# User stage in chunks of 20 history positions, transposed by VectorE in 32x32 blocks and placed by SBUF-to-SBUF DMAs, in place of groups of 4 positions transposed by TensorE

## The chip, the cores and the metric

The kernel runs on one core of one Trainium2 chip. The metric is the device time of one execution in microseconds (us); it was measured three times for the kernel before, between 31807.33 and 31812.54 us, with a median of 31807.57 us. One more execution was profiled, and all rows below come from that one.

The engines are named as in the profile: PE is TensorE (matrix products), PEld its loading of weights, DVE is VectorE, ACT is ScalarE, POOL is GpSimd, and SP is SyncE, which here only issues DMAs. A `q` behind an engine's name marks its sequencer, which issues a DMA while the engine itself stays idle.

## The reference, cut to what matters

```python
V = E[near_full]                       # 50001 items, 32 neighbours each
a_sus, a_inf = attention(E_in), attention(E_out)     # per item, over its neighbours
h = concat([E_hist[history], a_sus[history], a_inf[history]])   # 16384 x 100 x 128
t = concat([E_tgt[target], a_inf[target], a_sus[target]])       # 16384 x 128
x = h * t[:, None, :]
z = relu(einsum('bld,hd->blh', x, W1) + b1)                     # 128 -> 128
scores = einsum('blh,h->bl', z, W2[0])
exp_A = exp(scores) * ((history != target[:, None]) & (history != 0))
attn = exp_A / sum(exp_A, -1) ** 0.5
s = sum(h * attn[..., None])           # one number over everything
pred = dot(s, t) / (|s| * |t|);  return sigmoid(pred)
```

Everything is fp32. The output is one number for each of 16384 users.

## The kernel before, in words

There are two long stages and a short end.

**Neighbour stage** (lines 119 to 270). For each of 391 tiles of 128 items, POOL issues 32 indirect DMAs (line 161); each gathers one row of 64 numbers into each of 128 partitions, by an index that lies in SBUF. VectorE forms products (176), sums (183), weighted values (209) and weighted sums (217) in batches of two tiles; ScalarE takes the exponentials. The rows that result go to a table in HBM, 129 numbers for an item: the row's sum and the 128 numbers of `h`. The change leaves this stage as it is, save the width of the small constant `pick`.

**User stage** (lines 272 to 464). The users stand in 128 tiles of 128 (UC = 128), each user in a partition. A tile has 100 history positions, and for each of them one indirect DMA (line 343) gathers 128 rows of 516 bytes from the table, one for each partition. Four positions are a group (LG = 4), 25 groups make a tile, and step `s` runs over all 3200 groups:

- `gather(s)`: four indirect DMAs into the row buffer `rows[s % HB]`, one of HB = 6. The first waits until the transposes of step s - 6 have read that buffer.
- `sums(s)`: VectorE copies the four row sums to `hsum` (369), after the last of the four gathers has landed.
- `turn(s - 2)`: TensorE transposes four 128x128 blocks into PSUM (361).
- `times_target(s - 2)`: VectorE multiplies the PSUM block by the transposed target `tT` and writes `xT` to SBUF (378). One of its inputs lies in PSUM, the other in SBUF.
- `hidden`, `relu`, `scored`: TensorE multiplies by W1 (388), ScalarE takes the relu (394), TensorE picks the score of each position into a PSUM bank that collects the 25 groups (404).
- `weights`, `exponents`, `ended`: once per tile the bank is copied, transposed and passed through the exponential; four VectorE instructions of 100 columns mask and sum (428 to 431). Those on lines 428 and 430 have both inputs in SBUF, and so has line 333 of `target_work`.

`target_rows` gathers the target's rows for the next tile (310), `target_work` prepares the target, its sums and the mask (316 to 337).

**The order** on each engine is the order in which the code is written (`manual_schedule`), and each engine takes its instructions in turn. POOL carries no arithmetic: its queue is 12512 gathers on line 161, then 128 on line 310 among 12800 on line 343. Every gather signals its landing on one of eight semaphores in turn, and waits for the landing of the one eight places ahead of it. `after` adds a wait; `covered` drops one that a later wait or an engine's order makes needless.

Of the kernel before, what the change touches and what calls it, by code (L numbers as in the profile page):

```python
# [15 lines left out]
ALU = mybir.AluOpType  # L16
# [27 lines left out]
LG = 4  # L44
NG = L // LG
W = 1 + D
M = 2
HB = 6
RP = 3
LH = 3  # L50
LS = 6
LEAD = 2
XB = 5
ZB = 5

# [3 lines left out]
def kernel(  # L59
# [34 lines left out]
    pick = const.tile([HID, NG, NG], F32, name="pick")  # L94
# [26 lines left out]
    rows = [u_h.tile([P, LG, W], F32, name=f"h{i}") for i in range(HB)]  # L121
# [150 lines left out]
    with (  # L272
        tc.manual_schedule(engines={E.PE, E.Activation, E.DVE, E.SP, E.Pool}),
        tc.tile_pool(name="u_r", bufs=1) as u_r,
        tc.tile_pool(name="u_s", bufs=3) as u_s,
        tc.tile_pool(name="ps_r", bufs=1, space=bass.MemoryType.PSUM) as ps_r,
    ):
        users = {}
        landed, turned, times, first, second, third, copied = {}, {}, {}, {}, {}, {}, {}
        hT = [ps_r.tile([P, LG, P], F32, name=f"hT{i}") for i in range(RP)]  # L280
        z_ps = [ps_r.tile([HID, LG, P], F32, name=f"z_ps{i}") for i in range(RP)]
        writers, at = [], {}

        def next_bank():
            writers.append([])
            return hT[(len(writers) - 1) % RP]

        def writes(one):
            writers[-1].append(one)
            if len(writers) > RP:  # L290
                for other in writers[len(writers) - 1 - RP]:
                    covered(one, other)
            return one
        bank = [ps_r.tile([NG, LG, P], F32, name=f"bank{i}") for i in range(2)]
        xT = [u_r.tile([D, LG, P], F32, name=f"xT{i}") for i in range(XB)]
        z = [u_r.tile([HID, LG, P], F32, name=f"z{i}") for i in range(ZB)]
# [21 lines left out]
        def target_work(c):  # L318
            u = users[c]
            t = u["t"]  # L320
            tT_ps = next_bank()
            writes(nc.tensor.transpose(tT_ps[:, 0, :], t, ident))  # L322
            tT = u_t.tile([D, 1, P], F32, name="tT")
            nc.vector.tensor_copy(tT[:, 0, :], tT_ps[:, 0, :])
            u["tT"] = tT
            nc.vector.tensor_reduce(tsum[:, c : c + 1], t, AX.X, ALU.add)
            junk = u_t.tile([P, D], F32, name="junk")
            nc.scalar.activation(junk, t, AF.Square, accum_out=tsq[:, c : c + 1])
            keep = u_s.tile([P, L], F32, name="keep")
            idf = u_s.tile([P, L], F32, name="idf")  # L330
# [8 lines left out]
        def gather(s):  # L339
            c, g = divmod(s, NG)  # L340
            for q in range(LG):
                l = g * LG + q
                got = landed[s, q] = nc.gpsimd.indirect_dma_start(  # L343
                    out=rows[s % HB][:, q, :],
                    out_offset=None,
                    in_=table,
                    in_offset=bass.IndirectOffsetOnAxis(
                        ap=users[c]["hidx"][:, l : l + 1], axis=0
                    ),
                )  # L350
                if s >= HB:
                    if q == 0:
                        after(got, turned[s - HB, LG - 1])
                    if q < LG - 1:
                        covered(got, turned.pop((s - HB, q)))

        def turn(s):
            at[s] = next_bank()
            for q in range(LG):
                turned[s, q] = writes(  # L360
                    nc.tensor.transpose(at[s][:, q, :], rows[s % HB][:, q, 1:W], ident)  # L361
                )
            for q in range(LG):
                covered(turned[s, q], landed[s, q])
            after(turned[s, 0], copied[s])

        def sums(s):
            c, g = divmod(s, NG)
            copied[s] = copy = nc.vector.tensor_copy(  # L369
                users[c]["hsum"][:, g * LG : (g + 1) * LG],  # L370
                rows[s % HB][:, :, 0:1].rearrange("p q o -> p (q o)"),
            )
            for q in range(LG - 1):
                covered(copy, landed[s, q])

        def times_target(s):
            c, g = divmod(s, NG)
            times[s] = nc.vector.tensor_tensor(  # L378
                xT[s % XB], at.pop(s), users[c]["tT"].to_broadcast([D, LG, P]), ALU.mult
            )  # L380
            for q in range(LG - 1):
                covered(times[s], turned[s, q])
            if s >= XB:
                covered(times[s], times[s - XB])
                covered(times[s], first[s - XB])

        def hidden(s):
            first[s] = nc.tensor.matmul(z_ps[s % RP], w1T, xT[s % XB], start=True, stop=True)  # L388
            if s >= RP:
                covered(first[s], first[s - RP])  # L390
                after(first[s], second[s - RP])

        def relu(s):
            second[s] = nc.scalar.activation(z[s % ZB], z_ps[s % RP], AF.Relu, bias=b1_sb)  # L394
            if (s + LH + 1, LG - 1) in turned:
                covered(second[s], first[s])
                after(second[s], turned[s + LH + 1, LG - 1])
            if s >= ZB:
                covered(second[s], second[s - ZB])
                covered(second[s], third[s - ZB])  # L400

        def scored(s):
            c, g = divmod(s, NG)
            third[s] = nc.tensor.matmul(  # L404
                bank[c % 2], pick[:, g, :], z[s % ZB], start=g == 0, stop=g == NG - 1
            )

        def weights(c):
            flat = u_t.tile([NG, LG, P], F32, name="flat")
            copy = nc.scalar.copy(flat, bank[c % 2])  # L410
            for g in range(NG - 1):
                covered(copy, third[c * NG + g])
            users[c]["flat"] = flat

        def exponents(c):
            flat = users[c].pop("flat")
            score = next_bank()
            for q in range(LG):
                writes(nc.tensor.transpose(score[:, q, 0:NG], flat[:, q, :], ident[0:NG, 0:NG]))
            users[c]["ea"] = u_s.tile([P, L], F32, name="ea")  # L420
            nc.scalar.activation(
                users[c]["ea"].rearrange("p (g q) -> p q g", q=LG), score[:, :, 0:NG], AF.Exp
            )

        def ended(c):
            u = users.pop(c)
            ea = u["ea"]
# [5 lines left out]
        last = UC * NG  # L433
        target_rows(0)
        target_work(0)
        for s in range(last + LEAD + LS + 6):
            c, g = divmod(s, NG)
            if s < last:
                if g == 0 and c % BSUB == 2 and 0 < c // BSUB and c // BSUB + 1 < UC // BSUB:
                    history_of(c // BSUB + 1)  # L440
                if g == 5 and c + 1 < UC:
                    target_rows(c + 1)
                gather(s)
                sums(s)
            r = s - LEAD
            if 0 <= r < last:
                turn(r)
            if 0 <= r - LH < last:
                hidden(r - LH)
            if 0 <= r - LH - 1 < last:  # L450
                relu(r - LH - 1)
# [92 lines left out]
```

## Time and profile before

| what | us |
|---|---|
| median of three runs | 31807.57 |
| lowest and highest run | 31807.33, 31812.54 |
| span of the profiled execution, first to last instruction | 31804.2 |
| busy in that span: PE / DVE / ACT / POOL | 10552.2 / 6968.9 / 2748.7 / 24002.5 |
| mean granted TensorE clock | 0.907 |

The profiled execution's own time is known by its span; the median of the three runs lies 3.4 us above that span.

A row of the page reads: line, engine, operation, output<-inputs by the program's names, shape, count, then the busy time of all of them in us and the mean of one in ns, and behind the bar the engine's idle time just ahead of them with what ended most of it. "Issue" stands for an idle time in which the engine waited for nothing that the profile shows. A row of the timeline reads: start in us, duration in us, engine, line, operation, tiles, and in brackets the idle time just ahead of it.

### The profile page before, as it was taken

To read this page: it belongs to the slowest core of one execution; us is meant where nothing else is said; L and a number is where in the kernel's file an instruction comes from. 1 tells how busy PE (TensorE), PEld (TensorE's weight loads), DVE (VectorE), ACT (ScalarE), POOL (GpSimd) and SP (SyncE) were. 2 spreads that over 40 slices of the span, in tenths; PEclk is the share of its full clock that TensorE was granted. 3 is DMA by queue.
4 is the path that set the end of the run, shared out by engine and by line. 5 is a ranking of instruction groups with operands and counts; after the bars stand their busy time and mean duration, and the time that the engine had idled before them with its cause. 6 is when DMAs were issued, how large, how long until landed. Compare 5 with 4: busy or idle time off the path is not lost.

```text
span 31804.2 us, 99297 instructions
## 1 busy us (share of the span) xinstructions
PE 10552.2 (33%) x26243; PEld 3265.1 (10%) x26243; DVE 6968.9 (22%) x9965; ACT 2748.7 (9%) x5698; POOL 24002.5 (75%) x25446
## 2 busy tenths in 40 slices
PE   0000000000000000000166666666666666666666
PEld 0000000000000000000022222222222222222222
DVE  2222222222222222222211111111111111111111
ACT  0000000000000000000011111111111111111111
POOL 7777777777777777777777777777777777777777
PEclk9999999999999999999988888888888888888888
DMA  2111111111111111111122222222222222222222
GB/s 51 30 30 30 30 30 34 30 30 30 30 30 34 30 30 30 30 30 32 37 54 54 54 54 54 54 54 54 54 54 54 54 54 54 54 54 54 54 53 52
DMA packets 1027929, 1361.99 MB, mean 43 GB/s; under 512 B 559905, under 2 KB 614433, under 8 KB 1027361
## 3 DMA queue, kind: packets, MB, share of 16 engines
q0 software_dynamic: 814080, 1265.42, 16.5%
q1 hardware_dynamic: 112800, 51.60, 0.6%
q10 hardware_dynamic: 100480, 38.63, 0.6%
q8 instruction: 206, 3.38, 0.0%
q14 instruction: 363, 2.97, 0.0%
HBM read 1315.31 MB, written 51.50 MB: 43 GB/s over the span
## 4 chain that ended last, share of the span: by engine, by line
POOL 61%; issue 27%; DMA 12%; DVE 0%; POOLq 0%; PE 0%; ACT 0%; DVEq 0%; ACTq 0%
POOL v L161 36%; POOL h L343 25%; DMA h<-table,hidx 10%; DMA v<-in_egeo_dram,nidx 2%; POOL t L310 0%; POOLq L343 0%; DVE xT L378 0%; DVE den L429 0%; PE bank L404 0%; DVE ea L428 0%; PE z_ps L388 0%; DVE wv L209 0%; POOLq L161 0%; DMA nidx<-in_near_dram 0%; DVE hsum L369 0%
## 5 line engine op out<-in xcount | busy, mean ns | idle before, releaser
L343 POOL DMA_INDIRECT h<-table,hidx x12800 | 12076.8, 943 | 3901.3 <-issue 3493.5
L161 POOL DMA_INDIRECT v<-in_egeo_dram,nidx x12512 | 11804.3, 943 | 3820.7 <-issue 3756.2
L322 PE MATMUL hT<-ident,t 128*128 128x128 f32 x128 | 45.2, 353 | 15631.0 <-DMA t<-ttab,tidx 15631.0
L388 PE MATMUL z_ps<-xT,w1T 128*128 128x512 f32 x6400 | 4508.2, 796 | 0.0
L361 PE MATMUL hT<-ident,h 128*128 128x128 f32 x12800 | 2518.4, 329 | 5597.1 <-DVE hsum L369 4686.9
L404 PE MATMUL bank<-z,pick 128*25 128x512 f32 x6400 | 4231.8, 750 | 0.0
L369 DVE COPY hsum<-h 128x4 f32<-128x4 f32 x3200 | 616.7, 193 | 13349.4 <-DMA h<-table,hidx 13349.4
L394 ACT ACTIVATE z<-z_ps,b_sb 128x512 f32<-128x512 f32 x3200 | 2198.8, 687 | 13530.0 <-PE hT L361 13525.8
L176 DVE TENSOR_TENSOR prod<-v,own_ps 128x4096 f32<-128x4096 f32 x196 | 864.5, 4411 | 10996.4 <-DMA v<-in_egeo_dram,nidx 10996.4
L361 PEld LDWEIGHTS hT<-ident,h 128*128 128x128 f32 x12800 | 1597.8, 161 | 9101.8 <-DVE hsum L369 7555.2
L378 DVE TENSOR_TENSOR xT<-hT,tT 128x512 f32<-128x512 f32 x3200 | 2174.4, 680 | 0.0
L322 PEld LDWEIGHTS hT<-ident,t 128*128 128x128 f32 x128 | 18.9, 147 | 15774.4 <-issue 15772.8
L193 ACT ACTIVATE ex<-sc,top 128x32 f32<-128x32 f32 x782 | 227.7, 291 | 14840.8 <-DVE top L188 14821.9
L209 DVE TENSOR_TENSOR wv<-v,ex 128x1024 f32<-128x1024 f32 x782 | 1377.0, 1872 | 355.9 <-ACT ex L193 355.9
L388 PEld LDWEIGHTS z_ps<-xT,w1T 128*128 128x128 f32 x6400 | 1232.0, 239 | 2.6 <-ACT z L394 2.5
L183 DVE TENSOR_REDUCE sc<-prod 128x128 f32<-128x4096 f32 x196 | 864.4, 4410 | 6.7
L217 DVE TENSOR_REDUCE att<-wv 128x128 f32<-128x4096 f32 x196 | 864.1, 4409 | 6.1
L404 PEld LDWEIGHTS bank<-z,pick 128*25 128x25 f32 x6400 | 459.2, 115 | 3494.6 <-issue 3494.6
L310 POOL DMA_INDIRECT t<-ttab,tidx x128 | 120.7, 943 | 55.0 <-issue 37.5
L193 ACT ACTIVATION_READ_ACCUMULATOR ex<-sc,top 128x1 f32 x782 | 146.0, 187 | 0.0
L174 ACT COPY own_ps<-own 128x64 f32<-128x64 f32 x391 | 82.3, 210 | 60.4 <-DVE row L235 54.3
L220 DVE TENSOR_TENSOR row<-att,tot 128x64 f32<-128x64 f32 x391 | 70.7, 222 | 6.7
(53 smaller groups left out, 789.7 us busy)
## 6 DMA issues: line engine op xcount, KB each, us to landing
h<-table,hidx POOLq DMA_INDIRECT x12800, 2.5
v<-in_egeo_dram,nidx POOLq DMA_INDIRECT x12512, 2.4
table<-row ACTq DMA_DIRECT2D x22, 1096.5 KB, 13.4
own<-in_egeo_dram SPq DMA_DIRECT2D x23, 544.0 KB, 8.4
row<-in_ehist_dram SPq DMA_DIRECT2D x23, 544.0 KB, 4.7
ttab<-in_etgt_dram ACTq DMA_DIRECT2D x1, 12500.0 KB, 54.1
ttab<-row SPq DMA_DIRECT2D x22, 544.0 KB, 4.4
hidx<-in_history_dram SPq DMA_DIRECT2D x32, 200.0 KB, 2.4
```

The costliest lines, as they stand in the source:

```text
L161: nc.gpsimd.indirect_dma_start(out=v[:, m, k].rearrange("p t d -> p (t d)"), out_offset=None, in_=egeo, in_offset=bass.IndirectOffsetOnAxi ...
L176: nc.vector.tensor_tensor(prod[:, 0:n].rearrange("p m k t d -> p m k (t d)"), v.rearrange("p m k t d -> p m k (t d)"), own_ps[:, 0:n].to_b ...
L183: nc.vector.tensor_reduce(sc[:, 0:n].rearrange("p m t k -> p m k t"), prod[:, 0:n], AX.X, ALU.add)
L209: nc.vector.tensor_tensor(wv[:, m, t].rearrange("p d k -> p k d"), subs[b]["v"][:, m, :, t, :], ex[:, m, t, :].rearrange("p (k o) -> p k o ...
L217: nc.vector.tensor_reduce(att[:, 0:n], wv[:, 0:n], AX.X, ALU.add)
L343: got = landed[s, q] = nc.gpsimd.indirect_dma_start(out=rows[s % HB][:, q, :], out_offset=None, in_=table, in_offset=bass.IndirectOffsetOn ...
L361: nc.tensor.transpose(at[s][:, q, :], rows[s % HB][:, q, 1:W], ident)
L369: copied[s] = copy = nc.vector.tensor_copy(users[c]["hsum"][:, g * LG : (g + 1) * LG], rows[s % HB][:, :, 0:1].rearrange("p q o -> p (q o)"),)
L378: times[s] = nc.vector.tensor_tensor(xT[s % XB], at.pop(s), users[c]["tT"].to_broadcast([D, LG, P]), ALU.mult)
L388: first[s] = nc.tensor.matmul(z_ps[s % RP], w1T, xT[s % XB], start=True, stop=True)
L394: second[s] = nc.scalar.activation(z[s % ZB], z_ps[s % RP], AF.Relu, bias=b1_sb)
L404: third[s] = nc.tensor.matmul(bank[c % 2], pick[:, g, :], z[s % ZB], start=g == 0, stop=g == NG - 1)
```

## The change

The user stage is written anew; the neighbour stage and the end stay. A step is now a chunk of 20 positions (LQ = 20), five for each tile of users, 640 in all.

- `gather(s)` issues the same indirect DMAs in the same order, 20 in a row, into one of three row buffers of 20 positions.
- `blocks(s)` has three VectorE instructions: `x = h * t` over 20 x 128 columns (343 of the new file; both inputs lie in SBUF, the target's row repeated over the 20 positions), the copy of 20 row sums (349), and one transpose of all 32x32 blocks of `x` into `xb` (357).
- `move(s)` has SyncE issue 16 DMAs within SBUF, each of 32 partitions times 640 columns, which put block (a, b) into its place in `xT`.
- `hidden`, `relu`, `scored` take groups of 512 columns as before, five for a chunk; `relu` takes two at once. TensorE transposes nothing in this stage any more.
- `weights`: VectorE transposes the bank of scores in 32x32 blocks, four DMAs place them; then the exponential and the same four VectorE instructions. The target is no longer transposed.

```diff
-LG = 4
-NG = L // LG
+LQ = 20
+NCH = L // LQ
+Q = 4
+GS = 32
+COLS = 512
+NG = L * P // COLS
+PER = NG // NCH
-HB = 6
-RP = 3
-LH = 3
-LS = 6
-LEAD = 2
-XB = 5
-ZB = 5
+HB = 3
+XB = 2
+ZB = 4
+LS = 4
...
-    rows = [u_h.tile([P, LG, W], F32, name=f"h{i}") for i in range(HB)]
+    rows = [u_h.tile([P, LQ, W], F32, name=f"h{i}") for i in range(HB)]
...
-                if s >= HB:
-                    if q == 0:
-                        after(got, turned[s - HB, LG - 1])
...
+        def blocks(s):
+            c, k = divmod(s, NCH)
+            u = users[c]
+            h = rows[s % HB]
+            x = u_x.tile([P, LQ, D], F32, name="x")
+            made = nc.vector.tensor_tensor(
+                x,
+                h[:, :, 1:W],
+                u["t"].rearrange("p (o d) -> p o d", o=1).to_broadcast([P, LQ, D]),
+                ALU.mult,
+            )
+            copy = nc.vector.tensor_copy(
+                u["hsum"][:, k * LQ : (k + 1) * LQ], h[:, :, 0:1].rearrange("p q o -> p (q o)")
+            )
...
+            xb = xbs[s % XB]
+            turn = nc.vector.transpose(
+                xb.rearrange("p b q j -> p q b j"), x.rearrange("p q (b i) -> p q b i", b=Q)
+            )
+            if s >= XB:
+                after(copy, first.pop(s - XB))
...
+        def move(s):
+            xb = turned.pop(s)
+            xT = u_m.tile([D, Q, LQ * GS], F32, name="xT")
+            went[s] = [
+                nc.sync.dma_start(
+                    xT[b * GS : (b + 1) * GS, a, :],
+                    xb[a * GS : (a + 1) * GS, b].rearrange("p q j -> p (q j)"),
                 )
+                for b in range(Q)
+                for a in range(Q)
+            ]
...
         def weights(c):
-            flat = u_t.tile([NG, LG, P], F32, name="flat")
-            copy = nc.scalar.copy(flat, bank[c % 2])
...
+            flat = u_t.tile([GS, COLS], F32, name="flat", bufs=2)
+            nc.vector.transpose(
+                flat.rearrange("p (g n) -> p n g", g=GS), bank.pop(c).rearrange("p (n j) -> p n j", j=GS)
+            )
+            score = u_s.tile([P, L], F32, name="score")
+            of = flat[:, 0 : Q * L].rearrange("p (k a q) -> p k a q", k=NCH, a=Q)
+            for a in range(Q):
+                nc.sync.dma_start(
+                    score[a * GS : (a + 1) * GS, :].rearrange("p (k q) -> p k q", k=NCH), of[:, :, a, :]
+                )
```

Two places show how the instructions move. The first is VectorE in the middle of the user stage. Before, a group of four positions takes two instructions; `h_97` to `h_102` are the six row buffers, `hT` the PSUM block with the transposed rows, and the brackets name the semaphores that the instruction waits for (DMASW: landing of a gather).

```order
L369 COPY hsum<-h_101 128x4 [waits DMASW7_49]
L378 TENSOR_TENSOR xT_18221<-hT_18211,tT 128x512 [waits PE_49]
L369 COPY hsum<-h_102 128x4 [waits DMASW3_49]
L378 TENSOR_TENSOR xT_18217<-hT_18209,tT 128x512 [waits PE_49]
L369 COPY hsum<-h_97 128x4 [waits DMASW7_49]
```

In the changed kernel a chunk of 20 positions takes three; `h_98` and `h_99` are two of the three row buffers, `t` the target's rows, and the four rows on 435 to 438 come once per tile of users.

```order
L343 TENSOR_TENSOR x<-h_98,t 128x2560 [waits DMASW4_49]
L349 COPY hsum<-h_98 128x20 [waits PE_49]
L357 STREAM_TRANSPOSE xb_18223<-x 128x20x4x32 [waits DVE_49]
L435 TENSOR_TENSOR ea<-ea,keep 128x100 [waits Activation_49]
L436 TENSOR_REDUCE den<-ea 128x1 [waits DVE_49]
L437 TENSOR_TENSOR ea<-ea,hsum 128x100 [waits DVE_49]
L438 TENSOR_REDUCE num<-ea 128x1 [waits DVE_49]
L343 TENSOR_TENSOR x<-h_99,t 128x2560 [waits DMASW0_49]
```

The product that waited for TensorE and read PSUM now waits for the landing of the chunk's last gather and reads SBUF twice; it has 2560 columns in place of 512.

The second place is POOL's queue, at the same number of instructions from its start. Before, every fourth gather waits for VectorE and TensorE, besides the landing of the gather eight places ahead:

```order
L343 DMA h_102<-table,hidx 128x129 [waits DMASW5_49]
L343 DMA h_97<-table,hidx 128x129 [waits DMASW6_49,DVE_49,PE_49]
L343 DMA h_97<-table,hidx 128x129 [waits DMASW7_49]
L343 DMA h_97<-table,hidx 128x129 [waits DMASW0_49]
L343 DMA h_97<-table,hidx 128x129 [waits DMASW1_49]
L343 DMA h_98<-table,hidx 128x129 [waits DMASW2_49,DVE_49,PE_49]
```

In the changed kernel (line 329 is its gather):

```order
L329 DMA h_99<-table,hidx 128x129 [waits DMASW5_49]
L329 DMA h_97<-table,hidx 128x129 [waits DMASW6_49,DVE_49]
L329 DMA h_97<-table,hidx 128x129 [waits DMASW7_49]
...
L329 DMA h_97<-table,hidx 128x129 [waits DMASW1_49]
L329 DMA h_98<-table,hidx 128x129 [waits DMASW2_49,DVE_49]
```

The gathers stand in the same order with the same eight landing semaphores; the wait for VectorE comes once in 20 of them, and none waits for TensorE.

More of the change, by code (lines that the diff above doesn't have):

```diff
@@ L367, in sums @@
[L367 to L371, printed above, removed]
-            )
[L373 to L379, printed above, removed]
-            )
[L381 to L400, printed above, removed]
@@ new lines, in relu, with scored @@
+        def relu(pair):
+            zs[pair] = zr[pair % ZB]
+            second[pair] = nc.scalar.activation(zs[pair], hid.pop(pair), AF.Relu, bias=b1_sb)
+            if pair >= ZB:
+                covered(second[pair], second.pop(pair - ZB))
+                covered(second[pair], third.pop(2 * (pair - ZB)))
+                covered(second[pair], third.pop(2 * (pair - ZB) + 1))
+        def scored(n):
+            c, g = divmod(n, NG)
+            if g == 0:
+                bank[c] = ps_s.tile([GS, COLS], F32, name="bank")
+            third[n] = nc.tensor.matmul(
+                bank[c], pick[:, g, :], zs[n // 2][:, n % 2, :], start=g == 0, stop=g == NG - 1
+            )
+            if n % 2 == 1:
+                zs.pop(n // 2)
```

151 lines of the change are left out of this document (69 added, 82 removed).

## The prediction

> **What bounds the kernel now.** I read the page first: span, busy times, chain, then the costliest groups.
>
> ```profile
> span 31804.2 us, 99297 instructions
> PE 10552.2 (33%) x26243; PEld 3265.1 (10%) x26243; DVE 6968.9 (22%) x9965; ACT 2748.7 (9%) x5698; POOL 24002.5 (75%) x25446
> POOL 61%; issue 27%; DMA 12%; DVE 0%; POOLq 0%; PE 0%; ACT 0%; DVEq 0%; ACTq 0%
> L343 POOL DMA_INDIRECT h<-table,hidx x12800 | 12076.8, 943 | 3901.3 <-issue 3493.5
> L161 POOL DMA_INDIRECT v<-in_egeo_dram,nidx x12512 | 11804.3, 943 | 3820.7 <-issue 3756.2
> L310 POOL DMA_INDIRECT t<-ttab,tidx x128 | 120.7, 943 | 55.0 <-issue 37.5
> ```
>
> The chain of waits holds almost nothing but gathers. A gather on line 343 costs (12076.8 + 3901.3) / 12800 = 1.248 us, one on line 161 (11804.3 + 3820.7) / 12512 = 1.249 us: 0.943 us busy and 0.305 us in which POOL waits for nothing shown. The three lines together are 31,779 of the 31,804 us. So the kernel is POOL's queue from end to end, TensorE is idle two thirds of the time, and work that is taken off TensorE is worth nothing. The gathers stay as many. The question is whether the new work changes 1.248 us.
>
> **Can other work slow a gather?** In the timeline of the neighbour stage long VectorE instructions run across several gathers:
>
> ```profile
> 15587.63 4.42 DVE L176 TENSOR_TENSOR prod<-v,own_ps 128x4096 f32<-128x4096 f32 x1 [56.44 <-DMA v<-in_egeo_dram,nidx]
> 15590.18 0.94 POOL L161 DMA_INDIRECT v<-in_egeo_dram,nidx  x1 [0.30 <-issue]
> 15591.43 0.94 POOL L161 DMA_INDIRECT v<-in_egeo_dram,nidx  x1 [0.30 <-issue]
> ```
>
> 4.42 us of VectorE leave the step at 1.25 us. But `own_ps` lies in PSUM, so only one input comes from SBUF. With both in SBUF the trace before has only short ones, lines 428, 430 and 333. This is the stretch of the timeline where two of them meet a gather:
>
> ```profile
> 24032.56 0.94 POOL L343 DMA_INDIRECT h<-table,hidx  x1 [0.30 <-issue]
> 24032.60 0.17 DVE L369 COPY hsum<-h 128x4 f32<-128x4 f32 x1 [4.24 <-DMA h<-table,hidx]
> ...
> 24033.28 0.25 DVE L428 TENSOR_TENSOR ea<-ea,keep 128x100 f32<-128x100 f32 x1
> ...
> 24033.81 0.94 POOL L343 DMA_INDIRECT h<-table,hidx  x1 [0.31 <-DMA h<-table,hidx]
> 24033.86 0.26 DVE L430 TENSOR_TENSOR ea<-ea,hsum 128x100 f32<-128x100 f32 x1
> ```
>
> In the middle of a gather (428, while the one of 24032.56 runs) both go at full speed. Where the same instructions start just ahead of a gather, it is another picture:
>
> ```profile
> 17478.00 0.34 DVE L430 TENSOR_TENSOR ea<-ea,hsum 128x100 f32<-128x100 f32 x1
> 17478.04 0.94 POOL L343 DMA_INDIRECT h<-table,hidx  x1 [0.30 <-issue]
> ...
> 24112.40 0.24 DVE L369 COPY hsum<-h 128x4 f32<-128x4 f32 x1 [4.15 <-DMA h<-table,hidx]
> 24112.44 0.94 POOL L343 DMA_INDIRECT h<-table,hidx  x1 [0.30 <-issue]
> ...
> 29959.28 0.32 DVE L430 TENSOR_TENSOR ea<-ea,hsum 128x100 f32<-128x100 f32 x1
> 29959.31 0.95 POOL L343 DMA_INDIRECT h<-table,hidx  x1 [0.30 <-issue]
> ```
>
> Line 430 takes 0.32 to 0.34 us in place of 0.26, the copy 0.24 in place of 0.17: about 0.07 us more, and the gather loses nothing. A gather thus holds for a moment at its start something that a copy from SBUF to SBUF and a product of two SBUF tiles need too; I take it to be the reading of its indices through a port shared with VectorE. Here POOL came first. VectorE came first in one place, where 333 had been running for 0.18 us when a gather started:
>
> ```profile
> 15646.66 0.32 DVE L333 SCALAR_TENSOR_TENSOR keep<-idf,tidf,keep 128x100 f32<-128x100 f32 x1
> 15646.84 0.96 POOL L343 DMA_INDIRECT h<-table,hidx  x1 [0.69 <-issue]
> 15648.11 0.94 POOL L343 DMA_INDIRECT h<-table,hidx  x1 [0.31 <-issue]
> ```
>
> That gather took 0.96 us in place of 0.94, and came 0.39 us late besides. It ended its hold about when 333 was through. One case is thin, but it is what a port would do that the first comer keeps until it has finished.
>
> A rule of the Trainium skill goes further than these rows (SBUF — State Buffer, section "SBUF: two separate sides"): the port pair that VectorE and GpSimd share is an exclusive lock held for the whole instruction, and a VectorE instruction with two SBUF inputs takes it against a GpSimd operation that reads SBUF. By that rule the new product would hold up every gather that starts under it, as in the forecast below. Another page (Perfetto Trace Analysis, section "DMA Instruction — SWDGE (GPSIMD)") says that DMAs issued from GpSimd read no tensor; by it the product would hold up nothing, as in rival 1. The lengthened 430 speaks for the first page: something of the gather does use the port.
>
> **The change part by part.**
>
> *The product, line 343 of the new file: two SBUF inputs, 2560 columns, 640 times.*
>
> ```profile
> L378 DVE TENSOR_TENSOR xT<-hT,tT 128x512 f32<-128x512 f32 x3200 | 2174.4, 680 | 0.0
> L176 DVE TENSOR_TENSOR prod<-v,own_ps 128x4096 f32<-128x4096 f32 x196 | 864.5, 4411 | 10996.4 <-DMA v<-in_egeo_dram,nidx 10996.4
> ```
>
> A column costs (4411 - 680) / 3584 = 1.041 ns. From 430 (0.26 us for 100 columns) the product takes 0.26 + 2460 x 1.041 ns = 2.82 us. It starts when the chunk's last gather lands; before, the copy on 369 started on the same signal and, as at 24032.60 and 24112.40, within 0.05 us of a gather's start. So: a gather starts at 0 and reads its indices first, the product begins (0.05 to 0.1 us late) and runs to about 2.85; the next gather is due at 1.25. If it must wait for the product, less about 0.1 us at its end (in the case of 333, gather and instruction overlapped by 0.14 us at a cost of 0.02), it comes at 2.8 and POOL loses 1.55 us. Bounds: nothing below, as no gather of a queue with equal steps can come earlier; above, the whole 2.82 us, if the product is first or stops the gather under way too. The rows nearest to it are 333 and 430, which wait for one another; I take 1.55. The last chunk has no gather behind it: 639 x 1.55 = **990 us**.
>
> *The copy of 20 sums and the transpose of 2560 columns.* The copy came 3200 times and comes 640 times; each time a gather and it met, the copy paid. The transpose has no row before. It reads one tile, as 176 does from SBUF, and I take the same 2.8 us and no cost to POOL; bounds 0 and 2.8 us a chunk if it holds the port as well. VectorE then has some 5.9 us of work in a chunk of 20 x 1.25 = 25 us.
>
> *16 moves a chunk, issued by SyncE.*
>
> ```profile
> 763.17 0.57 SPq L146 DMA_DIRECT2D row<-in_ehist_dram  x1
> h<-table,hidx POOLq DMA_INDIRECT x12800, 2.5
> hidx<-in_history_dram SPq DMA_DIRECT2D x32, 200.0 KB, 2.4
> ```
>
> 16 x 0.57 = 9 us to issue and 2.4 us for the last to land, beside the next chunk's gathers; even 1.2 us apiece would be 19 of 25 us. A move waits for an earlier move, VectorE, or TensorE three chunks back; behind it in SyncE's queue stand only moves and the scores, so nothing of POOL's. What the 1.3 MB could do is delay landings: each gather waits for the one eight ahead, 8 x 1.25 = 10 us after a landing that takes 2.5. The neighbour stage shows a denser burst (view of the DMAs from 3464 to 3482 us, then the timeline):
>
> ```profile
> q1 hardware_dynamic: 3686, 1.70, 35.6%
> q10 hardware_dynamic: 2192, 1.12, 31.8%
> v<-in_egeo_dram,nidx POOLq DMA_INDIRECT x15, 6.1
> 3478.53 0.94 POOL L161 DMA_INDIRECT v<-in_egeo_dram,nidx  x1 [0.73 <-DMA v<-in_egeo_dram,nidx]
> ```
>
> 2.8 MB within 18 us bring landings to 6.1 us and cost one gather 0.43 us; the duration stays 0.94. Half of that in 25 us stays under 10 us: cost 0, bound above 0.43 x 640 = 275 us.
>
> *TensorE and ScalarE* lose the transposes and keep the rest: 0 to the time, as neither is waited for. *POOL's waits* for VectorE reach back three chunks, 75 us: 0.
>
> *The end of the program.*
>
> ```profile
> 31779.28 0.94 POOL L343 DMA_INDIRECT h<-table,hidx  x1 [0.30 <-issue]
> 31786.47 1.13 PE L388 MATMUL z_ps<-xT,w1T 128*128 128x512 f32 x2
> 31787.53 1.04 PE L404 MATMUL bank<-z,pick 128*25 128x512 f32 x2
> 31795.61 0.26 DVE L431 TENSOR_REDUCE num<-ea 128x1 f32<-128x100 f32 x1
> ```
>
> From the last gather to the end it was 31804.2 - 31779.3 = 24.9 us. Now: landing 2.5, three VectorE instructions 5.9, moves 11.4, ten products of TensorE with the relu about 12 (one on 388 and one on 404 take 2.2 us together), scores transposed and moved 5.5, exponential and sums 1.5, the unchanged rest 8.4: 47 us, **+22 us** (10 to 40).
>
> Sum: 31804.2 + 990 + 22 = 32,816 us by the profiled execution; the runs' median lies 3.4 us higher, so **32,820 us**, +3.2%.
>
> **The rivals.**
>
> 1. *No wait at all: the gather takes precedence whenever it comes, also in the middle of a VectorE instruction, and VectorE pays.* For it: in every row but one POOL lost nothing. Against: the 0.39 us and 0.02 us at 333. It decides if a gather that starts in the middle of the product keeps its step of 1.25 us. Time: 31,807.6 + 22 = 31,830 us, no change. Chance 0.17.
> 2. *The product is first more often, or stops the gather under way.* Then a chunk costs nearly 2.7 us: 639 x 2.7 = 1,725, 33,555 us. For it: the start of the copy lies within 0.05 us of the gather's, so little decides. Against: 428 in mid-gather left it at 0.94. Chance 0.06.
> 3. *The transpose holds the port too.* Another 1.6 us: 639 x 3.15 = 2,013, 33,840 us. Chance 0.05.
> 4. *The moves delay landings past 10 us*: at 0.43 us a chunk 32,105 us without the lock. Chance 0.04.
>
> **How the numbers follow.** The forecast has 0.66; with 1.4 to 1.8 us a chunk it gives 32,650 to 33,000. A gain has 0.02, since nothing in POOL's queue gets shorter. Runs of this kernel tell 0.2%, some 64 us, from no change; the forecast and rivals 2 to 4 are slower by more (0.81), rival 1 lies within (0.17). The range reaches from rival 1 over rival 4 to the upper end of the forecast, 31,815 to 33,050, and leaves out rivals 2 and 3. The forecast's own range is 32,650 to 33,000.
>
> **What would show it.** In the timeline of the changed kernel: one gather in each 20, the second to start after the chunk's last landing, late or long by about 1.5 us, with the product running ahead of it; all others at 1.25; line 329's busy and idle time together at 1.25 + 1.55 / 20 = 1.33 us a gather. Rival 1 shows a product of 2.9 us and gathers all at 1.25; rival 2 a loss of 2.7 us; rival 3 a second late gather under the transpose; rival 4 idle time ended by a landing. The prediction is wrong if the reading of indices isn't what the 0.07 us were, or if the delay of 0.39 us at 333 had another cause.

## The result, and the profile after

| | us |
|---|---|
| before, median of 4 runs (lowest, highest) | 31808.33 (31807.33, 31812.54) |
| changed, median of 4 runs (lowest, highest) | 32872.72 (32870.56, 32879.54) |
| ratio, 95% interval | 1.0335 (1.0321 to 1.035) |
| span of the profiled execution, changed | 32877.4 |

The changed kernel is 1,064 us slower. These are the rows of its page that answer to those of before: engines, chain, costliest groups.

```profile
PE 7953.0 (24%) x12803; PEld 1644.9 (5%) x12803; DVE 8237.3 (25%) x5485; ACT 2251.1 (7%) x3970; POOL 25051.8 (76%) x25446
POOL 72%; issue 24%; DMA 2%; PE 1%; SPq 0%; DVE 0%; ACT 0%; POOLq 0%; ACTq 0%; DVEq 0%
L329 POOL DMA_INDIRECT h<-table,hidx x12800 | 13126.7, 1026 | 3901.3 <-issue 3887.0
L162 POOL DMA_INDIRECT v<-in_egeo_dram,nidx x12512 | 11803.6, 943 | 3820.6 <-issue 3763.7
L343 DVE TENSOR_TENSOR x<-h,t 128x2560 f32<-128x2560 f32 x640 | 1808.6, 2826 | 10342.3 <-DMA h<-table,hidx 10342.3
L357 DVE STREAM_TRANSPOSE xb<-x 128x2560 f32<-128x2560 f32 x640 | 1821.0, 2845 | 0.0
L435 DVE TENSOR_TENSOR ea<-ea,keep 128x100 f32<-128x100 f32 x128 | 34.0, 266 | 2815.5 <-ACT ea L429 2815.5
```

The neighbour stage (162) is what it was. The user stage's gathers have the same idle time as before, 3901.3 us, but their **busy** time rose from 12076.8 to 13126.7 us: +1,049.9 us, nearly the whole difference. Nothing on the page calls it a wait. POOL stood in the gather itself.

The timeline shows where. First a chunk as most are, then one whose product stands behind the four instructions on 435 to 438:

```profile
24024.48 0.95 POOL L329 DMA_INDIRECT h<-table,hidx  x1 [0.30 <-issue]
24024.49 2.84 DVE L343 TENSOR_TENSOR x<-h,t 128x2560 f32<-128x2560 f32 x1 [21.98 <-DMA h<-table,hidx]
24025.73 2.42 POOL L329 DMA_INDIRECT h<-table,hidx  x1 [0.30 <-issue]
24027.26 0.17 DVE L349 COPY hsum<-h 128x20 f32<-128x20 f32 x1
24027.37 2.85 DVE L357 STREAM_TRANSPOSE xb<-x 128x2560 f32<-128x2560 f32 x1
24028.46 0.94 POOL L329 DMA_INDIRECT h<-table,hidx  x1 [0.31 <-issue]
24029.70 0.94 POOL L329 DMA_INDIRECT h<-table,hidx  x1 [0.30 <-issue]
...
24077.92 0.26 DVE L435 TENSOR_TENSOR ea<-ea,keep 128x100 f32<-128x100 f32 x1 [21.26 <-ACT ea L429]
...
24078.62 0.97 POOL L329 DMA_INDIRECT h<-table,hidx  x1 [0.30 <-issue]
24078.80 0.26 DVE L438 TENSOR_REDUCE num<-ea 128x1 f32<-128x100 f32 x1
24078.98 2.81 DVE L343 TENSOR_TENSOR x<-h,t 128x2560 f32<-128x2560 f32 x1
24079.89 2.71 POOL L329 DMA_INDIRECT h<-table,hidx  x1 [0.31 <-issue]
```

The gather of 24025.73 starts on time, 1.25 us after the one ahead of it, and then lasts 2.42 us. It ends at 24028.15, 0.82 us behind the product's end at 24027.33. In the second place it is 24082.60 against 24081.79: 0.81 us. The gathers under the transpose (24028.46, 24029.70) last 0.94 us.

Counted over the whole trace: 645 of the 12,800 gathers last over 1 us, and their excess is 1,050 us. Of 659 gathers that start under a running product 639 are lengthened, one for each product but the last; in the middle nine tenths of them the gather ends 0.813 to 0.821 us behind the product. The 20 others start within 0.041 us of the product's start. Of 1,278 gathers that start under a transpose none is lengthened. The six that are left of the 645 start under 435 or 437, which have both inputs in SBUF as well.

### The profile page after: what moved, and what is told of

Same layout as the page of the kernel before. It is cut to its first block, busy times and chain, and to the rows that moved or that the text cites. A ratio compares the mean times of both kernels' runs of the same rounds, so it can differ in the third digit from the quotient of the medians.

```text
span 32877.4 us, 77610 instructions
## 1 busy us (share of the span) xinstructions
PE 7953.0 (24%) x12803; PEld 1644.9 (5%) x12803; DVE 8237.3 (25%) x5485; ACT 2251.1 (7%) x3970; POOL 25051.8 (76%) x25446
## 4 chain that ended last, share of the span: by engine, by line
POOL 72%; issue 24%; DMA 2%; PE 1%; SPq 0%; DVE 0%; ACT 0%; POOLq 0%; ACTq 0%; DVEq 0%
POOL h L329 37%; POOL v L162 35%; DMA v<-in_egeo_dram,nidx 1%; DMA h<-table,hidx 1%; SPq L371 0%; POOL t L301 0%; PE z_ps L384 0%; PE bank L407 0%; DVE x L343 0%; DVE xb L357 0%; DMA xT<-xb 0%; ACT z L397 0%; DVE wv L210 0%; DMA nidx<-in_near_dram 0%; POOLq L162 0%
## 5 line engine op out<-in xcount | busy, mean ns | idle before, releaser
L329 POOL DMA_INDIRECT h<-table,hidx x12800 | 13126.7, 1026 | 3901.3 <-issue 3887.0
L343 DVE TENSOR_TENSOR x<-h,t 128x2560 f32<-128x2560 f32 x640 | 1808.6, 2826 | 10342.3 <-DMA h<-table,hidx 10342.3
L407 PE MATMUL bank<-z,pick 128*32 128x512 f32 x6400 | 3882.0, 693 | 0.0
L397 ACT ACTIVATE z<-z_ps,b_sb 128x1024 f32<-128x1024 f32 x1600 | 1781.4, 1113 | 15373.8 <-PE z_ps L384 15296.2
L357 DVE STREAM_TRANSPOSE xb<-x 128x2560 f32<-128x2560 f32 x640 | 1821.0, 2845 | 0.0
L435 DVE TENSOR_TENSOR ea<-ea,keep 128x100 f32<-128x100 f32 x128 | 34.0, 266 | 2815.5 <-ACT ea L429 2815.5
L407 PEld LDWEIGHTS bank<-z,pick 128*32 128x32 f32 x6400 | 472.2, 115 | 3089.1 <-issue 2412.5
L415 DVE STREAM_TRANSPOSE flat<-bank 32x512 f32<-32x512 f32 x128 | 125.8, 983 | 25.3 <-PE bank L407 25.3
L349 DVE COPY hsum<-h 128x20 f32<-128x20 f32 x640 | 108.4, 169 | 0.0
```

Source lines behind the costliest of these rows:

```text
L329: landed[s, q] = nc.gpsimd.indirect_dma_start(out=rows[s % HB][:, q, :], out_offset=None, in_=table, in_offset=bass.IndirectOffsetOnAxis(a ...
L343: made = nc.vector.tensor_tensor(x, h[:, :, 1:W], u["t"].rearrange("p (o d) -> p o d", o=1).to_broadcast([P, LQ, D]), ALU.mult,)
L357: turn = nc.vector.transpose(xb.rearrange("p b q j -> p q b j"), x.rearrange("p q (b i) -> p q b i", b=Q))
L397: second[pair] = nc.scalar.activation(zs[pair], hid.pop(pair), AF.Relu, bias=b1_sb)
L407: third[n] = nc.tensor.matmul(bank[c], pick[:, g, :], zs[n // 2][:, n % 2, :], start=g == 0, stop=g == NG - 1)
```

## The experiments

The twelve runs fell on four chips, and these differ. On one the kernel before took 31,846 us, close to the 31,808 above; on the other three, called slow chips below, 35,824, 35,929 and 35,914 us. Times are therefore compared within a chip only. What lengthens a gather can be counted on each of them. The counts are of the gathers of the user stage, the 128 of the targets among them; the excess is what the gathers over 1 us last beyond the 0.94 us of the others.

### The pair once more

Both kernels unchanged, side by side on another chip.

> The kernel before, profiled on the chip of this trial. If the chip is like the first (31,808 us): gathers at 1.25 us in both stages. If it is like the two of the experiments (35,824 and 35,929 us): some 17,510 us up to the end of the neighbour stage, as in all traces of those chips, and 18,300 us in the user stage; the question is whether its gathers are lengthened there (which is POOL's or the DMA's own doing) or wait for VectorE and TensorE (whose answers come late on these chips).

> The changed kernel, profiled on the same chip. Theory (port): in any trace of it, one gather in 20 is under way while a product runs and is lengthened from 0.94 to about 2.5 us; on a chip like the first that is 1,050 us and 32,873 us in all. On a chip like the two of the experiments the same lengthened gathers come with waits for VectorE on top, and the ratio to the kernel before, 1.022 to 1.032 for its variants there, tells nothing of the port alone. Rival (the loss on the first chip was its own): no lengthened gathers here.

The kernel before took 31,847.15 us, the changed one 32,883.13 us: +1,036 us, close to the 1,064 of the result, and near the forecast. The groups on POOL, the kernel before first:

```profile
L343 POOL DMA_INDIRECT h<-table,hidx x12800 | 12095.0, 945 | 3900.9 <-issue 3883.5 <-DMA h<-table,hidx 15.8 <-DVE tsum L326 0.6
```

```profile
L329 POOL DMA_INDIRECT h<-table,hidx x12800 | 13125.3, 1025 | 3901.2 <-issue 3889.0 <-DMA h<-table,hidx 12.2
```

Again the busy time of the gathers makes the difference (+1,030 us); 641 of them are over 1 us. So the loss was not peculiar to the first chip.

### The target in PSUM

```diff
-        tc.tile_pool(name="ps_r", bufs=3, space=bass.MemoryType.PSUM) as ps_r,
+        tc.tile_pool(name="ps_r", bufs=2, space=bass.MemoryType.PSUM) as ps_r,
...
+        tc.tile_pool(name="ps_t", bufs=2, space=bass.MemoryType.PSUM) as ps_t,
...
+            u["tp"] = ps_t.tile([P, 1, D], F32, name="tp")
+            nc.scalar.copy(u["tp"][:, 0, :], t)
...
-                u["t"].rearrange("p (o d) -> p o d", o=1).to_broadcast([P, LQ, D]),
+                u["tp"].to_broadcast([P, LQ, D]),
```

The product keeps its length and its place, and reads one input from SBUF and one from PSUM. The relu's PSUM buffers went from three to two to make room.

> The changed kernel with one edit: ScalarE copies the target's rows to PSUM once per tile of users, and the product reads them there, so only one of its inputs lies in SBUF (TensorE's PSUM buffers go from three to two to make room). Theory (port): a two-SBUF instruction of VectorE keeps a port that a gather needs at its start, so without it no gather waits: all steps at 1.25 us, 31,808 + 24 us of longer end = 31,832 us, 31,815 to 31,860. Rival (moves): the 16 DMAs a chunk slow the gathers: the time stays near 32,870. Rival (length): any VectorE instruction of 2.8 us, the transpose too, stops a gather: 32,850 or more, since product and transpose last as long as before.

> The product with the target's rows in PSUM once more, as the chip of the first trial needed 35,824 us for the kernel before, where every earlier run needed 31,808, and its stalls hid the effect in the time; in its trace no gather was lengthened any more. Where the kernel before takes 31,808 us: theory (port) 31,832 us (31,815 to 31,860), all gathers at 1.25 us; rival (moves, or the length of VectorE's instructions) 32,850 us or more.

> The targets that the product multiplies by are copied to PSUM by ScalarE, and the product reads them there, so that it has one input in SBUF and one in PSUM; all else, the moves and the transposes too, stays as in the changed kernel, but the PSUM buffers of the relu's rows go from three to two. Theory (a VectorE instruction with two inputs in SBUF makes the gather that is due wait to its end): no gather of the user stage waits, each step is 1.248 us, and where the kernel before takes 31,808 to 31,850 us this one takes 24 us more (the longer end of the program), 31,830 to 31,880. Rival (the moves' transfers, or the length of VectorE's instructions whatever they read, cost the 1,050 us): 32,850 or more. On a chip where the kernel before takes some 35,800 us the time tells nothing of this; there the theory gives about 40 gathers of the user stage that are busy over 1 us, the rival some 600.

Measured: 36,866.51 us where before took 35,823.77, ratio 1.0291 (1.0274 to 1.0308); 37,078.74 against 35,929.42, 1.0319 (1.0301 to 1.0336); 37,017.42 against 35,914.06, 1.0309 (1.0292 to 1.0326). All three fell on slow chips, and as times they decide nothing between the forecasts: the kernel before alone takes 4,000 us longer there than the forecasts assume. The gathers decide: 43, 39 and 39 of them are over 1 us, close to the 40 that the last expectation names for such a chip, with 10.7, 11.0 and 7.9 us in excess, where the changed kernel has 645 and 1,050. In the first of the runs 986 gathers of the history start under a running product, and 4 of these are lengthened. On the same chip a version whose product reads SBUF twice (the sums one chunk later, below) has 526 such gathers, and 523 are lengthened; its product lasts 2,794 ns too. From the third run, the costliest groups on POOL:

```profile
L162 POOL DMA_INDIRECT v<-in_egeo_dram,nidx x12512 | 13408.4, 1072 | 4081.2 <-issue 4005.7 <-DMA v<-in_egeo_dram,nidx 72.7 <-DMA nidx<-in_near_dram 2.8
L332 POOL DMA_INDIRECT h<-table,hidx x12800 | 12087.5, 944 | 7173.9 <-issue 3834.5 <-DVE hsum L352 3270.9 <-DVE x L346 58.2
```

The product's length is not what stops a gather, since it lasts about as long as ever (2,794 ns in the first and third runs), and the 16 moves, which stay, are not either: it is where the product's inputs lie. The rows also say why the time doesn't fall here. The neighbour stage, which no edit touches, has gathers of 1.072 us; and in the user stage POOL waits 3,271 us for the copy of sums on 352, a wait that the changed kernel's trace on the result's chip doesn't have. That copy is tied to TensorE's work of two chunks earlier.

### The product in five pieces

```diff
-            made = nc.vector.tensor_tensor(
-                x,
-                h[:, :, 1:W],
+            made = [
+                nc.vector.tensor_tensor(
+                    x[:, i : i + 4],
+                    h[:, i : i + 4, 1:W],
...
+                for i in range(0, LQ, 4)
+            ]
...
+                if q % 4 < 3:
+                    covered(made[q // 4], gone)
```

Five instructions of four positions, both inputs in SBUF: either each as soon as its own gathers have landed ("landing"), or all behind the chunk's last gather ("back", with `after(made[0], landed[s, LQ - 1])`).

> The changed kernel with the product cut into five of 4 positions (512 columns, some 0.69 us), each issued when its own four gathers have landed; both inputs stay in SBUF and the columns are as many. Theory (port): each piece begins within 0.1 us of a gather's start and ends at 0.8 us, before the next is due at 1.25; almost nothing is lost: 31,832 to 31,920 us. Rival (rate): two-SBUF work costs POOL in proportion to its time, wherever it lies: as the columns are the same and there are more instructions, 32,870 us or more.

> The same five pieces of 512 columns, but all issued behind the landing of the chunk's last gather, one straight after the other, some 3.1 us together. Theory (port, held for one instruction): the gathers due at 1.25 and 2.5 us wait for the end of the piece that runs, up to 0.6 us each, some 0.5 us a chunk: 32,150 us (31,900 to 32,500). Rival (held across instructions that follow straight on): 1.6 to 1.9 us a chunk, 32,870 to 33,080 us.

> The five pieces of 4 positions, each behind its own gathers, once more for the same reason. Where the kernel before takes 31,808 us: theory (port) 31,832 to 31,920 us, as a piece ends before the next gather is due; rival (two-SBUF work costs POOL in proportion to its time) 32,870 us or more.

> The product is made in five instructions of four positions, each as soon as its own four gathers have landed; all else as in the changed kernel. An estimate of one piece from the product's 2.826 us for twenty positions: 2.83 / 5 = 0.57 us and some fixed cost, so 0.6 us. Theory (the gather waits to the end of the instruction that it meets): a piece that starts behind a gather's start is over before the next gather is due 1.248 us later, so nearly nothing is lost; pieces that start late in a step cost at most 0.6 us each. Where the kernel before takes 31,808 to 31,850 us this takes 31,840 to 31,960. Rival (the loss goes by the elements that VectorE reads, however they are cut): 32,850 or more. On a chip where the kernel before takes some 35,800 us: lengthened gathers of about 0.4 us each, some 530 of them, as seen there.

Measured: 36,796.79 us, ratio 1.0273 (1.0256 to 1.029), and 36,785.02, 1.0267 (1.025 to 1.0284), beside the first run of the target in PSUM; 36,883.48, 1.0265 (1.0248 to 1.0282), and 36,872.4, 1.0267 (1.025 to 1.0284), on the two other slow chips. The times again decide nothing. Over 1 us are 541, 518, 533 and 512 gathers, with only 232, 225, 226 and 223 us in excess: 0.43 us each. Where one ends behind a piece, it is mostly 0.82 us behind that piece's end. The same 2,560 columns a chunk cost the gathers far less when the instruction that they meet is short, so the price is the rest of one instruction and not the columns read. Pieces behind the landing and pieces ahead of it can't be told apart here.

### The sums one chunk later

```diff
+            if 0 <= done < USERS and left == 2:
+                exped[done] = ended(done)
-            if 0 <= done < USERS and left == 2:
-                summed(done, ended(done))
+            if 0 <= done < USERS and left == 3:
+                summed(done, exped.pop(done))
```

The four instructions on 435 to 438 move behind another product, so that none starts late because of ScalarE's exponential.

> The changed kernel with the four masking and summing instructions of a tile issued one chunk later on VectorE, so that the product of the fourth chunk of each tile no longer stands behind their wait for ScalarE. In the changed kernel's trace the products of the other chunks begin 0.07 us after a gather's start and cost 1.53 us, those of the fourth begin at 0.73 us in the median and cost 2.09. Theory (port; the cost is set by how far into a step the product starts): 128 x 0.56 = 72 us less, 32,800 us (32,780 to 32,820). Rival: the cost of the fourth chunk comes from its other work, not from when its product starts: 32,870 us unchanged.

Measured, on the chip of the first run of the target in PSUM: 36,623.66 us, ratio 1.022 (1.0203 to 1.0237), and 607 gathers over 1 us with 1,316 us in excess, 2.17 us each. What the edit was for can't be read, since on that chip products start at any point of a step, because POOL and VectorE wait for other things. But the three versions on that one chip make a series: 2.17 us a gather with the whole product in SBUF, 0.43 with it in pieces, 0.25 (and only 43 of them) with one input in PSUM. The time runs the other way, 36,624, 36,785 to 36,797 and 36,867 us. **On such a chip the lengthened gathers are not what sets the end.**

### A later product, and a long copy

```diff
+            late = u_s.tile([P, 8], F32, name="late")
+            ahead = nc.vector.tensor_reduce(late, h[:, 12:LQ, 1:101], AX.X, ALU.add)
             made = nc.vector.tensor_tensor(
```

A reduction with one input goes ahead of the product, which then starts later in the step; its result is not used.

> The changed kernel with a sum over 800 columns ahead of each product (one input, some 1.0 us, waits for the same landing), so that the product starts some 1.0 us after a gather's start in place of 0.07; its result is not used. Theory (port; what counts is how long the product still runs when the next gather is due): the gather due at 1.25 waits until 3.75, 2.5 us in four chunks of five and about 2.1 in the fourth: 31,832 + 512 x 2.5 + 128 x 2.1 = 33,380 us (33,200 to 33,500). Rival (each two-SBUF product costs the same whenever it starts): 32,870 us.

One run: 37,501.85 us where before took 35,929.42: 435 gathers over 1 us, 834 us in excess. The timeline has both cases side by side:

```profile
24084.11 0.98 DVE L344 TENSOR_REDUCE late<-h 128x8 f32<-128x800 f32 x1
24084.53 0.95 POOL L329 DMA_INDIRECT h<-table,hidx  x1 [0.30 <-issue]
24085.01 2.81 DVE L345 TENSOR_TENSOR x<-h,t 128x2560 f32<-128x2560 f32 x1
24085.79 2.86 POOL L329 DMA_INDIRECT h<-table,hidx  x1 [0.30 <-issue]
...
24091.45 0.95 POOL L329 DMA_INDIRECT h<-table,hidx  x1 [0.30 <-issue]
24091.49 2.81 DVE L345 TENSOR_TENSOR x<-h,t 128x2560 f32<-128x2560 f32 x1
24092.70 2.42 POOL L329 DMA_INDIRECT h<-table,hidx  x1 [0.31 <-issue]
```

A product 0.48 us behind a gather's start makes the next one last 2.86 us, one 0.04 us behind makes it 2.42: a product that starts 0.44 us later costs 0.44 us more. By start in the step, over the run: median excess 1.48 us within the first 0.15 us, 1.92 from 0.4 to 0.7, 2.40 from 0.7 to 1.0.

The last edit adds to the target in PSUM a copy of the whole product, from SBUF to SBUF, and its result is not used either:

```diff
+            again = u_x.tile([P, LQ, D], F32, name="again")
+            nc.vector.tensor_copy(again, x)
```

> The kernel with the target's rows in PSUM and, behind each product, a copy of its 2560 columns from SBUF to SBUF whose result is not used. It starts 2.8 us after a gather's start. Theory (a copy from SBUF to SBUF holds the port as well, since the short copies had to wait for gathers): if it takes 1.4 us, the gather due at 3.75 waits 0.4 us, 32,100 us; if it takes 2.8 us, 1.8 us a chunk, 32,980 us. Rival (such a copy gives way to gathers): 31,832 us. Rival (it stops the gather under way too): 1.3 us or more a chunk, and lengthened gathers that started ahead of it, 32,650 us or more.

One run: 37,272.09 us, 420 gathers over 1 us, 423 us in excess, where the same kernel without the copy had 39 and 11 on the same chip. One stretch of its timeline holds all kinds of VectorE instruction:

```profile
18162.38 2.81 DVE L346 TENSOR_TENSOR x<-h,tp 128x2560 f32<-128x2560 f32 x1
18163.09 0.95 POOL L332 DMA_INDIRECT h<-table,hidx  x1 [0.30 <-issue]
18164.34 0.94 POOL L332 DMA_INDIRECT h<-table,hidx  x1 [0.30 <-issue]
18165.22 1.50 DVE L353 COPY again<-x 128x2560 f32<-128x2560 f32 x1
18165.59 1.94 POOL L332 DMA_INDIRECT h<-table,hidx  x1 [0.31 <-issue]
18166.63 0.17 DVE L354 COPY hsum<-h 128x20 f32<-128x20 f32 x1
18166.72 2.84 DVE L362 STREAM_TRANSPOSE xb<-x 128x2560 f32<-128x2560 f32 x1
18167.84 0.95 POOL L332 DMA_INDIRECT h<-table,hidx  x1 [0.30 <-issue]
```

Under the product with an input in PSUM two gathers keep 0.95 and 0.94 us. Under the copy one lasts 1.94 us and ends at 18167.53, 0.81 us behind the copy's end. Under the transpose the next keeps 0.95. All 308 gathers that start under this copy are lengthened, and none of the 1,331 under the transposes. So "two inputs in SBUF" is not the whole condition: a copy with one input does it too, and it is quick for its 2,560 columns (1,511 ns, the transpose 2,837). The Trainium skill (SBUF — State Buffer, section "SBUF: two separate sides") gives both conditions: beside two SBUF inputs it names a two-port mode of VectorE, "which fp32 SBUF→SBUF `tensor_copy` triggers". The rows agree with both.

The copy also stops gathers that are already under way, as the second rival of the expectation had it, though only young ones:

```profile
17539.28 2.82 DVE L346 TENSOR_TENSOR x<-h,tp 128x2560 f32<-128x2560 f32 x1 [24.50 <-DMA h<-table,hidx]
17541.69 2.05 POOL L332 DMA_INDIRECT h<-table,hidx  x1 [0.30 <-issue]
17542.13 1.49 DVE L353 COPY again<-x 128x2560 f32<-128x2560 f32 x1
```

The gather starts under the product, 0.44 us ahead of the copy, and ends at 17543.74, 0.12 us behind the copy's end. The same holds for all 89 gathers that start under the product and up to 0.51 us ahead of the copy, and for none that starts earlier. A product with two SBUF inputs doesn't do this: it starts 0.07 us behind a gather's start (24024.48 in the result's timeline) and leaves that gather at 0.95 us. So the two kinds of instruction hold a gather up at different points of its course. What the gather does at each of them no run tells.

## Why the prediction was right

- **POOL's queue is the bound.** Right: 72% of the chain is POOL and 24% issue, and no gather of the history is shown waiting for another engine.
- **The gather waits to the product's end.** Right, and it carries the result: 639 products hold one gather each. The trace of the changed kernel gives the sum by itself, and the runs with the target in PSUM show that the gathers go free when nothing but the product's second input (and a PSUM buffer) changes. Of the two rules of the Trainium skill that the prediction weighed, the lock (SBUF — State Buffer, section "SBUF: two separate sides") agrees with these rows as far as the gather waits for VectorE; the other way round it doesn't hold for the whole instruction, since a product starts 0.07 us behind a gather's start and runs its usual 2.8 us. The other rule (Perfetto Trace Analysis, section "DMA Instruction — SWDGE (GPSIMD)"), by which such DMAs read no tensor, would have left the gathers at 0.94 us. Whether a gather needs the port to read its indices, as the prediction took it, or for something else at its start, no run tells.
- **The evidence at 333 was in part misread.** The prediction counted two things against rival 1, a gather that came 0.39 us late and one of 0.96 us. The first had another cause, which stays open: the third gather of the history has 0.69 us of idle time in all four traces of the two kernels on the two faster chips. In the second run of the changed kernel, line 319 (there in place of 333) had ended at 15650.48, that gather was due at 15650.66, and it came 0.39 us late all the same:

```profile
15649.42 0.94 POOL L329 DMA_INDIRECT h<-table,hidx  x1 [0.30 <-issue]
15650.16 0.32 DVE L319 SCALAR_TENSOR_TENSOR keep<-idf,tidf,keep 128x100 f32<-128x100 f32 x1
15651.05 0.95 POOL L329 DMA_INDIRECT h<-table,hidx  x1 [0.69 <-issue]
```

The 0.02 us fit what was found: 0.14 us of 333 were left at the gather's start, and less 0.13 of overlap that is 0.01. So the mechanism rested on 0.02 us in one gather and on the lengthened 430; that it came out right owes something to luck.
- **Its price of 1.55 us.** The product takes 2.826 us (predicted 2.82). It starts 71 to 86 ns (medians) behind a gather's start in four chunks of a tile's five, and costs 1.53 us there. The overlap of 0.1 us at the end is 0.944 - 0.818 = 0.13 us.
- **The term that was mis-sized: 639 x 1.55 = 990 us; it is 1,050 us.** The fourth chunk of each tile costs 2.09 us on average. Its product doesn't wait for a landing alone: it stands in VectorE's queue behind 435 to 438, and 435 waits for ScalarE's exponential on 429, so the product starts at any point of the step, median 0.73 us, as in the second half of the timeline above. The row of 435 (2815.5 us idle for ScalarE) shows the wait; the order printed ahead of the prediction showed the queue. Counted by chunk: 195.7 + 195.6 + 196.4 + 268.0 + 194.5 = 1,050 us.
- **Copy, transpose and moves at nothing.** Right. The transpose takes 2.845 us (taken as 2.8), and no gather lasts longer under it. The 16 moves are issued in 10.0 us, as against 9 (line 371 in the rows below). A gather lands in 2.6 us, as against 2.5.
- **The end of the program, +22 us.** From the last gather, the first row below, to the end it is 32877.4 - 32828.9 = 48.5 us, in place of 24.9: +23.6.

```profile
32828.86 0.94 POOL L329 DMA_INDIRECT h<-table,hidx  x1 [0.30 <-issue]
32831.52 2.83 DVE L343 TENSOR_TENSOR x<-h,t 128x2560 f32<-128x2560 f32 x1 [17.12 <-DMA h<-table,hidx]
32837.29 10.00 SPq L371 DMA_DIRECT2D xT<-xb  x16
32846.95 2.07 PE L384 MATMUL z_ps<-xT,w1T 128*128 128x512 f32 x2 [9.15 <-DMA xT<-xb]
32862.56 1.02 DVE L415 STREAM_TRANSPOSE flat<-bank 32x512 f32<-32x512 f32 x1 [25.34 <-PE bank L407]
```

- **What would show it.** 329's busy and idle time together are (13126.7 + 3901.3) / 12800 = 1.330 us, the figure forecast. The form was left open between late and long: it is long, 1,050 us of busy time and none of idle.
- **The sum.** 31804.2 + 1,050 + 23.6 = 32,877.8 us, the span being 32,877.4. The prediction's 32,816 lacked 60 us of the fourth chunk and some 2 us of the end; that the runs' median lies 4.7 us under this span, and not above it, gives 8 back. At the lower end of the forecast's own range 1.4 us a chunk would make 32,724 us by this sum, and not the 32,650 stated; the result lies above both.
- **The rivals.** Each of 639 products held a gather up, where rival 1 has none; the loss is not the whole 2.7 us of rival 2; rival 3's transposes hold nothing; and waits for a landing (rival 4) come to 14.3 us in the whole user stage.

What stays open: the target in PSUM was not met on a chip where the kernel before takes some 31,800 us. That it would come within some 24 us of the kernel before there follows from the sum, and wasn't measured. Nor is it known what makes three of the four chips slower, or what the change costs on these; the ratios there were 1.022 to 1.032 in all versions that ran four times, with and without lengthened gathers; the changed kernel itself was not among these.

## What to carry to other kernels

Where a queue of indirect gathers is the bound, work that "lies beside it" on VectorE is free only if it leaves the gathers alone: look at the mean duration of a gather as well as at its idle time. One input in PSUM, or shorter instructions, took most of the loss from the gathers in these runs; whether that gives time back has to be read on the chip at hand. And when a wait ends with another instruction, the point at which that instruction starts enters the price: look up what stands ahead of it in its queue, for each of the places where it comes.

## What was not expected of the hardware

- The wait of a gather for VectorE is recorded as the gather's own busy time (0.94 us becomes 2.42), with no idle time and no releaser; the chain of waits calls it POOL.
- A gather can be held up for a product that hasn't started yet. With the sums one chunk later, a product stands ready behind a transpose of scores on 415, which reads PSUM:

```profile
18371.72 1.03 DVE L415 STREAM_TRANSPOSE flat<-bank 32x512 f32<-32x512 f32 x1 [37.25 <-remote]
18371.86 4.36 POOL L329 DMA_INDIRECT h<-table,hidx  x1 [0.30 <-issue]
18372.61 2.78 DVE L343 TENSOR_TENSOR x<-h,t 128x2560 f32<-128x2560 f32 x1
```

The gather started 0.75 us ahead of the product and still ended 0.83 us behind it, 4.36 us long. So it is for all 70 gathers of this run that start under 415 and at most 0.83 us ahead of the product. It is no rule for every instruction that stands ready: of 208 gathers that start as shortly ahead of a product that follows straight on the transpose on 357, none is lengthened. With the target in PSUM the transpose of scores lengthens no gather. This was read from the rows and not tried by itself; why 415 differs from 357 stays open.

- Chips differ, or their state at the time, as each was met at one time only. Three of the four of the experiments took 12.6 to 13.0% longer for the kernel before than the result's 31,808 us; in the traces of the versions that ran there the gathers of the neighbour stage take 1.07 us on average in place of 0.94.
